# Node features of a graph kernel loaded on two queues, and the last rows of h stored on GpSimd's

## The chip, the cores and the metric

The kernel runs on one core of a Trainium2 chip. The metric is device microseconds (us) of one execution; below 4023 us, about 8 us are 0.2%. Engines are named as in the profile: PE is TensorE, DVE is VectorE, ACT is ScalarE, POOL is GpSimd, SP is SyncE. SPq and ACTq are the instruction queues of SP and ACT when they issue transfers.

## The reference, cut to what matters

One layer of a graph network with 12,500 nodes of 160 features (64 scalars, 32 vectors of 3 components) and 400,000 edges sorted by destination, then a residual and a layer norm.

```python
s = node_features[:, :64]; v = node_features[:, 64:].reshape(n, 32, 3)
h_s = s @ lin1_ws * a / sqrt(64)                                 # the table h, one row of 160 a node
h_v = einsum('nci,cd->ndi', v, lin1_wv) * a / sqrt(32)
w = silu(edge_scalars @ fc_w1 / sqrt(64)) @ fc_w2 / sqrt(64)     # 224 weights an edge
es, ev = h_s[edge_src], h_v[edge_src]                            # gathered by the edge's source
# messages: products of w, es, ev and edge_attr; summed by the edge's destination
# lin2 on the sums + a self connection -> gates -> out
x = layernorm(x + out)
```

Every edge needs the finished row of h of its source node, which can be any of the 12,500.

## The kernel before

**Set-up.** The table h is built in seven chunks of up to 2048 nodes (`CH`; `starts` holds their first nodes; the last chunk has 212). `load(c0)` (L229) loads a chunk, feature by feature, in three transfers: 64 scalar rows of 8 KB into partitions 0 to 63 of `xa` (512 KB, L235), the first 64 of the 96 rows of vector components into partitions 64 to 127 of `xa` (512 KB, L236), and the other 32 as four quarters into 128 partitions of `xz` (256 KB, L241). All three are issued by SP. ACT's queue brings the node attribute `at` (L249), the block-diagonal weights `l1` (L253, L256) and `l1z` (L277, four small strided transfers) and one row of destinations (L282). ACT also scales `l1` and `l1z` (L280).

The chunk loop (L309) does for each chunk: 16 matmuls with `l1` into the PSUM tiles `hp` (L320; 32 in the trace, since the profile shows two passes of a float32 matmul), four with `l1z` into `pz` (L336), and on DVE five multiplications by the attribute into `ht` (L323, L339). `hp` has six buffers, `ht` three, so a chunk's `ht` waits for the store of the chunk three before. POOL stores the chunk to the DRAM table `h_tab` (L350). Ahead of the fourth chunk, `bases()` (L292) computes each block's first destination on DVE, spreads it over the partitions by PE, and ACT copies it out of three `hp` buffers (L304). The last chunk is one full tile of 128 nodes, stored by POOL (L350), and 84 rows more, stored by SP (L353).

After the loop POOL issues the first edge scalars `es` (L196) and all destinations `dt` (L357); DVE scales `w2` (L364), computes the relative destinations `rel` (L398) when `dt` has landed, and runs `scale()` (L259) over the output weights, which SP loads at L368 to L391.

**Edge loop.** 782 steps of up to four tiles of 128 edges. POOL issues one indirect transfer a tile, which gathers 128 rows of `h_tab` into `hg` (L452; buffers for four steps). PE makes the edge weights (L443, L465), DVE the products (L475, L483) and the selection (L528, L537), PE adds them up by destination (L544), and closed blocks go through lin2 and the output steps. The order on PE, DVE, ACT and POOL is the order of the program text; SP's is too during the set-up (`tc.manual_schedule`). Transfers issued by SP and ACT share eight semaphores in turn, so a transfer waits until the one that last used its semaphore has landed.

Of the kernel before, what the change touches and what calls it, by code (L numbers as in the profile page):

```python
# [10 lines left out]
F32 = mybir.dt.float32  # L11
# [9 lines left out]
P = 128  # L21
S = 64
V = 32
# [30 lines left out]
def gnn_kernel(  # L54
# [21 lines left out]
    nc = tc.nc  # L76
# [10 lines left out]
    consts = ctx.enter_context(tc.tile_pool(name="consts", bufs=1))  # L87
    dram = ctx.enter_context(tc.tile_pool(name="dram", bufs=1, space=bass.MemoryType.DRAM))
    h_tab = dram.tile([N, D], F32, name="h_tab")
# [69 lines left out]
    def index(t):  # L159
        a0, idx, _ = ahead(t)  # L160
        return idx[:, t - a0:t - a0 + 1]
# [20 lines left out]
    def in_pairs(a):  # L182

        return a.rearrange("o (c k h) -> o h c k", k=KB, h=2)
# [11 lines left out]
            queue.dma_start(to[:, :n * P], es_t[:, e0:e0 + n * P])  # L196


    ident = consts.tile([P, P], F32, name="ident")
    make_identity(nc, ident)  # L200
    iota_i = consts.tile([P, W], I32, name="iota_i")
# [21 lines left out]
    starts = list(range(0, N, CH))  # L223
    with tc.tile_pool(name="nodes", bufs=len(starts)) as nodes, tc.tile_pool(
        name="nodes_ps", bufs=6, space=PSUM
    ) as nps, tc.tile_pool(name="z_ps", bufs=2, space=PSUM) as zps:
        loaded = []

        def load(c0):  # L229

            cn = min(CH, N - c0)
            quarters = 4 if cn == CH else 1
            assert quarters == 4 or cn <= U * P
            xa = nodes.tile([P, CH], F32, name="xa")
            nc.sync.dma_start(xa[:S, :cn], xs_t[:, c0:c0 + cn])  # L235
            nc.sync.dma_start(xa[S:, :cn], xv_t[:2 * V, c0:c0 + cn])  # L236
            xz = nodes.tile([P, U * P], F32, name="xz")
            cq = cn // quarters
            z = xv_t[2 * V:, c0:c0 + cq]
            if quarters == 4:  # L240
                nc.sync.dma_start(xz[:, :cq], bass.AP(tensor=z.tensor, offset=z.offset,  # L241
                                                      ap=[[z.ap[0][0], V], [cq, 4], [1, cq]]))
            else:
                nc.sync.dma_start(xz[S:S + V, :cq], z)
            loaded.append((c0, cn, quarters, cq, xa, xz))

        load(starts[0])
        at = consts.tile([P, NT], F32, name="at")
        nc.scalar.dma_start(at, attr)  # L249

        l1 = consts.tile([P, P], F32, name="l1")
        nc.vector.memset(l1, 0.0)
        nc.scalar.dma_start(l1[:S, :S], lin1_ws)  # L253
        for i in range(2):
            r = slice(S + i * V, S + (i + 1) * V)
            nc.scalar.dma_start(l1[r, r], lin1_wv)  # L256
        scales = [(l1[:S], 1.0 / math.sqrt(S)), (l1[S:], 1.0 / math.sqrt(V))]

        def scale():  # L259
            for m, by in scales:  # L260
                nc.vector.tensor_scalar_mul(m, m, by)
            scales.clear()

        def block_diagonal(name, w, n, scale, queue=nc.scalar):
            k = w.shape[0]
            m = consts.tile([n * k, n * k], F32, name=name)
            nc.vector.memset(m, 0.0)
            for i in range(n):
                queue.dma_start(m[i * k:(i + 1) * k, i * k:(i + 1) * k], w)
            if scale != 1.0:  # L270
                scales.append((m, scale))
            return m

        l1z = consts.tile([P, P], F32, name="l1z")
        nc.vector.memset(l1z, 0.0)
        for q in range(4):
            nc.scalar.dma_start(l1z[q:q + 4 * V - 3:4, q * V:(q + 1) * V], lin1_wv)  # L277
        scales.append((l1z, 1.0 / math.sqrt(V)))
        for m, by in scales:
            nc.scalar.mul(m, m, by)  # L280
        scales.clear()
        nc.scalar.dma_start(dt[0:1], dst[0:1])  # L282
        for c0 in starts[1:]:
            load(c0)
        index(0)
        raw = ends_pool.tile([2 * S, NWT], F32, name="raw")
        for half in range(2):
            r = slice(half * S, (half + 1) * S)
            nc.sync.dma_start(w1[r, r], fc_w1)
            nc.sync.dma_start(raw[r], fc_w2)  # L290

        def bases():  # L292

            firsts = dt[0:1, 0:(even - 1) * BT + 1:BT].rearrange("o (c h k) -> o h c k", k=KB, h=2)
            for half in range(2):
                nc.vector.tensor_copy(in_pairs(rows[:, :even])[:, half], firsts[:, half])
            nc.vector.tensor_copy(rows[:, even:], dt[0:1, even * BT:(NB - 1) * BT + 1:BT])
            base_f = ends_pool.tile([1, NB], F32, name="base_f")
            nc.vector.tensor_copy(base_f, rows)
            for b0 in range(0, NB, U * P):  # L300
                b1 = min(NB, b0 + U * P)
                ps = nps.tile([P, U, P], F32, name="hp").rearrange("p u c -> p (u c)")
                nc.tensor.matmul(ps[:, :b1 - b0], ones, base_f[:, b0:b1], start=True, stop=True)
                nc.scalar.copy(lo[:, b0:b1], ps[:, :b1 - b0])  # L304
            nc.vector.tensor_sub(share, rows, share)
            nc.vector.tensor_reduce(early, share, AX.X, OP.min)
            nc.vector.tensor_scalar(early, early, -float(MARGIN), None, op0=OP.is_lt)

        for c0, cn, quarters, cq, xa, xz in loaded:  # L309
            if c0 == 3 * CH:  # L310
                bases()
            ht = nodes.tile([P, 4 * U, D], F32, name="ht", bufs=3)
            nt = -(-cn // P)
            first = c0 // P
            full = cn // P
            for t0 in range(0, nt, U):
                ps = nps.tile([P, U, P], F32, name="hp")
                for t in range(t0, min(t0 + U, nt)):
                    n = min(P, cn - t * P)
                    nc.tensor.matmul(ps[:n, t - t0], xa[:, t * P:t * P + n], l1,  # L320
                                     start=True, stop=True)
                k = min(U, full - t0)
                nc.vector.tensor_mul(  # L323
                    ht[:, t0:t0 + k, :P], ps[:, :k],
                    at[:, first + t0:first + t0 + k, None].to_broadcast([P, k, P]))
                if t0 + k < nt <= t0 + U:
                    n = cn - full * P
                    nc.vector.tensor_scalar(ht[:n, full, :P], ps[:n, full - t0],
                                            at[:n, first + full:first + full + 1], None, op0=OP.mult)

            pz = zps.tile([P, U, 4, V], F32, name="pz")
            r = slice(0, P) if quarters == 4 else slice(S, S + V)
            by = l1z if quarters == 4 else l1[r, r]
            for u in range(-(-cq // P)):
                n = min(P, cq - u * P)
                nc.tensor.matmul(pz[:n, u, :quarters].rearrange("p q c -> p (q c)"),  # L336
                                 xz[r, u * P:u * P + n], by, start=True, stop=True)
            if quarters == 4:
                nc.vector.tensor_mul(  # L339
                    ht[:, :, P:].rearrange("p (q u) c -> p u q c", q=4), pz,  # L340
                    at[:, first:first + 4 * U].rearrange("p (q u) -> p u q", q=4)[:, :, :, None]
                    .to_broadcast([P, U, 4, V]))
            else:
                nc.vector.tensor_mul(ht[:, :full, P:], pz[:, :full, 0],
                                     at[:, first:first + full, None].to_broadcast([P, full, V]))
            if cn > full * P:
                n = cn - full * P
                nc.vector.tensor_scalar(ht[:n, full, P:], pz[:n, full, 0],
                                        at[:n, first + full:first + full + 1], None, op0=OP.mult)
            nc.gpsimd.dma_start(  # L350
                h_tab[c0:c0 + full * P, :].rearrange("(q p) d -> p q d", p=P), ht[:, :full])
            if cn > full * P:
                nc.sync.dma_start(h_tab[c0 + full * P:c0 + cn, :], ht[:n, full])  # L353


    load_chunk(0, nc.gpsimd)
# [26 lines left out]
    for to, part, pieces, w, r0, c0, by in maps:  # L383
        for k, piece in enumerate(pieces):
# [3 lines left out]
            m = terms.setdefault((to, part, four), len(terms))  # L388
# [267 lines left out]
    with tc.tile_pool(  # L656
        name="fin", bufs=1
    ) as fin, tc.tile_pool(
        name="late", bufs=2
    ) as late, tc.tile_pool(name="edge", bufs=2) as edge, tc.tile_pool(  # L660
        name="deep", bufs=4
# [150 lines left out]
        with tc.manual_schedule(engines={ENG.PE, ENG.DVE, ENG.Activation, ENG.Pool}):  # L812
# [47 lines left out]
            n = len(steps)  # L860
# [138 lines left out]
```

## Time and profile before

| | |
|---|---|
| three runs | 4021.55, 4023.07, 4029.47 us; median 4023.07 |
| the profiled execution | 4018.78 us, of which the span of the profile is 4017.0 us |
| granted PE clock, mean over the span | 0.967 |
| busy | PE 3676.3 us (92%), POOL 2982.9 (74%), DVE 2410.5 (60%), ACT 938.7 (23%) |
| gathers (L452) | 3125, each 950 ns; the first starts at 65.42 us, the last at 3984.85 us |

Times are us from the start of the span unless marked ns. In the list of instruction groups a line gives the source line, engine, operation, output<-input, count, then busy time and mean ns of one, then the idle time just before them and what ended most of it. In the timeline a line gives the start, the time taken, engine, line, operation, tiles, and in brackets the idle time before it with what released it. A row of DMA_DIRECT2D is the issue of a transfer and not its data; a transfer's landing is its semaphore's last update in the trace. In the table of stretches a line gives the stretch and its length, each engine's busy time with its number of instructions, the granted PE clock, the mean busy share of the 16 DMA engines, and GB/s.

### The profile page before, as it was taken

The page shows a single profiled execution, that of the slowest core. Times are in us where ns is not written, and L with a number is a line of the kernel's source. Part 1 is how long each engine was busy: PE and PEld are TensorE (multiplying, and loading weights), DVE is VectorE, ACT ScalarE, POOL GpSimd, SP SyncE. Part 2 cuts the span into 40 slices and gives each one's busy share as a digit, 9 for nine tenths or more (in the row PEclk, how much of TensorE's full clock was granted, in tenths as well). Part 3 has the DMA queues.
Part 4 walks back from the last instruction along what each step waited for, and adds up shares of the span by engine and source line. Part 5 has one row for each costly group of instructions (what it writes and reads, how often), then busy time and mean ns, then how long its engine had stood idle before and what let it go on. Part 6 is the DMA issues. An engine that isn't in the chain of part 4 may idle for free. (4 is left out here: it accounts for less than half of the span.)

```text
span 4017.0 us, 46675 instructions
## 1 busy us (share of the span) xinstructions
PE 3676.3 (92%) x14291; PEld 1588.0 (40%) x14291; DVE 2410.5 (60%) x6596; ACT 938.7 (23%) x2463; POOL 2982.9 (74%) x3144
## 2 busy tenths in 40 slices
PE   6899899999999999999999999999899989999997
PEld 4344343343343433334333443344343334333443
DVE  5556565655655655656656655666565665655655
ACT  2222222221222222212212222222121221222222
POOL 4777777777777777777777777777777777777775
PEclk8999999999999999999999999999999999999999
DMA  8444444443444444444444444444444444444442
GB/s 240 95 100 98 98 104 96 103 106 94 101 102 98 103 98 102 103 100 101 101 99 100 95 106 101 96 106 99 98 105 95 105 102 95 103 101 98 100 96 58
DMA packets 227691, 411.71 MB, mean 102 GB/s; under 512 B 71883, under 2 KB 157383, under 8 KB 226535
## 3 DMA queue, kind: packets, MB, share of 16 engines
q0 software_dynamic: 152272, 266.53, 27.9%
q1 hardware_dynamic: 74646, 142.01, 14.7%
q8 instruction: 115, 1.88, 0.2%
q14 instruction: 144, 1.18, 0.1%
q10 hardware_dynamic: 514, 0.10, 0.0%
HBM read 392.41 MB, written 16.00 MB: 102 GB/s over the span
## 5 line engine op out<-in xcount | busy, mean ns | idle before, releaser
L452 POOL DMA_INDIRECT hg<-h_tab,idx x3125 | 2968.7, 950 | 962.2 <-issue 865.5
L465 PE MATMUL pw<-w,hid 128*128 128x448 f32 x3126 | 1376.5, 564 | 191.5 <-DVE sel L537 150.1
L544 PE MATMUL pa<-pr,sel 128*64 128x416 f32 x6250 | 1303.5, 539 | 0.0
L475 DVE TENSOR_TENSOR pr<-pw,hg 128x512 f32<-128x512 f32 x782 | 540.5, 691 | 1042.4 <-DMA hg<-h_tab,idx 784.2
L483 DVE TENSOR_TENSOR pr<-pw,hg 128x384 f32<-128x384 f32 x2346 | 1153.6, 547 | 0.0
L465 PEld LDWEIGHTS pw<-w,hid 128*128 128x128 f32 x3126 | 556.3, 195 | 685.8 <-issue 445.3
L544 PEld LDWEIGHTS pa<-pr,sel 128*64 128x64 f32 x6250 | 388.0, 139 | 812.3 <-issue 799.4
L740 ACT COPY sa<-pa 128x416 f32<-128x416 f32 x521 | 263.1, 505 | 1415.4 <-PE pa L544 1413.0
L443 PE MATMUL misc<-es,w 128*128 128x512 f32 (+1 forms) x784 | 448.0, 654 | 17.0 <-DMA es<-in_es_t_dram 14.3
L528 DVE TENSOR_TENSOR pw<-rel,iota 128x64 f32<-128x64 int16 x782 | 178.4, 228 | 468.3 <-PE pw L465 465.5
L445 ACT ACTIVATE hid<-misc 128x512 f32<-128x512 f32 x392 | 233.5, 596 | 743.9 <-PE misc L443 743.4
L553 PEld LDWEIGHTS misc<-ident,sa 128*128 128x128 f32 x2084 | 239.6, 141 | 311.6 <-issue 252.1
L568 PE MATMUL misc<-tt,l 128*96 128x256 f32 (+5 forms) x1496 | 346.0, 378 | 1.7 <-ACT tt L558 1.5
L553 PE MATMUL misc<-ident,sa 128*128 128x128 f32 x2084 | 328.1, 280 | 0.9 <-DVE acc L721 0.8
L537 DVE TENSOR_TENSOR sel<-pw,eas 128x256 f32<-128x256 f32 x782 | 323.6, 414 | 0.0
L556 ACT COPY tt<-misc 128x192 f32<-128x192 f32 x521 | 164.5, 316 | 517.2 <-PE misc L553 516.7
L568 PEld LDWEIGHTS misc<-tt,l 128*96 128x96 f32 (+1 forms) x1496 | 227.0, 162 | 139.6 <-issue 72.6
L443 PEld LDWEIGHTS misc<-es,w 128*128 128x128 f32 x784 | 119.2, 191 | 283.2 <-issue 228.5
L576 DVE TENSOR_TENSOR acc<-acc,os 96x32 f32 x1042 | 195.6, 188 | 23.9 <-ACT os L571 5.5
L603 PE MATMUL misc<-ident,acc 96*128 96x96 f32 x196 | 36.4, 272 | 90.7 <-DVE pw L528 41.8
L558 ACT COPY tt<-misc 128x64 f32<-128x64 f32 x521 | 117.1, 225 | 0.0
L571 ACT COPY os<-misc 96x512 f32<-96x512 f32 (+2 forms) x68 | 38.3, 563 | 303.1 <-PE misc L568 280.4
(84 smaller groups left out, 653.0 us busy)
## 6 DMA issues: line engine op xcount, KB each, us to landing
es<-in_es_t_dram SPq DMA_DIRECT2D x258, 384.0 KB
hg<-h_tab,idx POOLq DMA_INDIRECT x3125
h_tab<-ht POOLq DMA_DIRECT2D x6, 1280.0 KB
xt<-in_x_dram SPq DMA_DIRECT2D x23, 320.0 KB
out_dram<-y SPq DMA_DIRECT2D x23, 320.0 KB
xv<-in_xv_t_dram SPq DMA_DIRECT2D x25, 187.5 KB
xs<-in_xs_t_dram SPq DMA_DIRECT2D x25, 125.0 KB
xa<-in_xs_t_dram SPq DMA_DIRECT2D x6, 512.0 KB
```

What stands on the lines that cost most here:

```text
L443: nc.tensor.matmul(ph[:k, c], w1[:k, :k], es[:k, t0 * P + c0 * P:t0 * P + c1 * P], start=True, stop=True)
L445: nc.scalar.activation(hid[:k, c], ph[:k, c], AF.Silu, scale=1.0 / math.sqrt(64))
L452: nc.gpsimd.indirect_dma_start(out=hg[:, t, :], out_offset=None, in_=h_tab, in_offset=bass.IndirectOffsetOnAxis(ap=i, axis=0))
L465: nc.tensor.matmul(pw[:, t:t + m, :NWT], hid[:m * S, c * P:(c + 1) * P], w2[:m * S, :m], start=True, stop=True)
L475: nc.vector.tensor_mul(two, pw[:, :n, :2 * S].rearrange("p t (k c) -> p t k c", k=2), hg[:, :n, None, :S].to_broadcast([P, n, 2, S]))
L483: nc.vector.tensor_mul(pr[:, :n, first:first + V3].rearrange("p t (i c) -> p t i c", i=3), pw[:, :n, None, 2 * S + k * V:2 * S + (k + 1) * ...
L537: nc.vector.tensor_mul(sel[:, :n], oh[:, :, None, :].to_broadcast([P, n, 4, W]), by_slot(tiles[0][0])[:, u:u + n, :, None].to_broadcast([P ...
L544: nc.tensor.matmul(pa[half * ROWS:(half + 1) * ROWS, :NPR], sel[:, t].rearrange("p k w -> p (k w)"), pr, start=start, stop=stop)
L553: nc.tensor.transpose(pt[:, four * P:four * P + k], sa[:k, c:c + P], ident[:k, :k])
L568: nc.tensor.matmul(po[:, k, :nb], l2[r, terms[to, part, four]], a[:, :nb], start=(n == 0), stop=(n == len(of) - 1))
L576: nc.vector.tensor_add(window, window, os[:, :, b])
L740: nc.scalar.copy(sa, pas.pop(j)[:, :NPR])
```

## The change

It has five edits. The vector half of `xa` is issued by ACT where SP issued it. `l1` and `l1z` are allocated and cleared at the head of the set-up. `l1` is scaled by `scale()` on DVE just ahead of the chunk loop; `l1z` stays with ACT, now after the second chunk's load. The loads of the other chunks follow that. The 84 last rows of h are stored by POOL right after the tile before them.

```diff
+    l1 = consts.tile([P, P], F32, name="l1")
+    l1z = consts.tile([P, P], F32, name="l1z")
+    for m in (l1, l1z):
+        nc.vector.memset(m, 0.0)
     ident = consts.tile([P, P], F32, name="ident")
...
             nc.sync.dma_start(xa[:S, :cn], xs_t[:, c0:c0 + cn])
-            nc.sync.dma_start(xa[S:, :cn], xv_t[:2 * V, c0:c0 + cn])
+            nc.scalar.dma_start(xa[S:, :cn], xv_t[:2 * V, c0:c0 + cn])
...
-        l1 = consts.tile([P, P], F32, name="l1")
-        nc.vector.memset(l1, 0.0)
         nc.scalar.dma_start(l1[:S, :S], lin1_ws)
...
-        l1z = consts.tile([P, P], F32, name="l1z")
-        nc.vector.memset(l1z, 0.0)
         for q in range(4):
             nc.scalar.dma_start(l1z[q:q + 4 * V - 3:4, q * V:(q + 1) * V], lin1_wv)
-        scales.append((l1z, 1.0 / math.sqrt(V)))
-        for m, by in scales:
-            nc.scalar.mul(m, m, by)
-        scales.clear()
         nc.scalar.dma_start(dt[0:1], dst[0:1])
-        for c0 in starts[1:]:
+        load(starts[1])
+        nc.scalar.mul(l1z, l1z, 1.0 / math.sqrt(V))
+        for c0 in starts[2:]:
             load(c0)
...
+        scale()
         for c0, cn, quarters, cq, xa, xz in loaded:
...
             if cn > full * P:
-                nc.sync.dma_start(h_tab[c0 + full * P:c0 + cn, :], ht[:n, full])
+                nc.gpsimd.dma_start(h_tab[c0 + full * P:c0 + cn, :], ht[:n, full])
```

## The prediction, made before the change was run

> **What bounds the kernel now.** I read the list of groups first, then who waited for whom on POOL, then the timeline of the first 85 us, then the DMA rate by stretch. The group that matters is the gather:
>
> ```profile
> L452 POOL DMA_INDIRECT hg<-h_tab,idx x3125 | 2968.7, 950 | 962.2 <-issue 865.5
> ```
>
> Each gather takes 950 ns and about 0.30 us of idle stands before it. POOL's waits, longest first, say what that idle is:
>
> ```profile
> POOL hg L452 <- issue: 865.5, 2841, 0.3
> ...
> POOL hg L452 <- DMA h_tab<-ht: 10.5, 1, 10.5
> ```
>
> The columns are total us, times, longest. No wait of a gather is longer than 0.3 us except the very first, which waited 10.5 us for h. The starts of the 3125 gathers run from 65.42 to 3984.85 us, a mean step of 1.2546 us, and the products (L483) free a gather's buffers at least 4.8 us before POOL needs them (81.81 against 86.58 us at the fifth step, the tightest of all). So PE's 92% does not set the pace: POOL's issue does, from the first gather to the last, and 31.2 us of output steps follow (4017.0 less 3984.85 and 0.95). This change touches nothing inside that loop. Its worth is how far it moves the first gather from 65.42 us, and 0.2%, about what a measurement of this kernel can tell from no change, is 8.0 us. The timeline shows what that start hangs on:
>
> ```profile
> 9.40 0.64 ACT L280 ACTIVATE l<-l 64x128 f32<-64x128 f32 x2
> 10.09 5.78 PE L320 MATMUL hp<-l,xa 128*128 128x128 f32 x32 [10.09 <-ACT l L280]
> 17.26 3.81 PE L320 MATMUL hp<-l,xa 128*128 128x128 f32 x32 [0.49 <-DMA xa<-in_xv_t_dram]
> 22.89 3.81 PE L320 MATMUL hp<-l,xa 128*128 128x128 f32 x32 [0.93 <-DVE ht L339]
> 41.77 1.15 POOL L350 DMA_DIRECT2D h_tab<-ht  x1 [11.87 <-DVE ht L339]
> 50.70 1.15 POOL L350 DMA_DIRECT2D h_tab<-ht  x1 [3.31 <-DVE ht L339]
> 52.71 0.56 POOL L350 DMA_DIRECT2D h_tab<-ht  x1 [0.85 <-DVE ht L348]
> 53.22 0.82 SPq L353 DMA_DIRECT2D h_tab<-ht  x1
> 65.42 1.04 POOL L452 DMA_INDIRECT hg<-h_tab,idx  x1 [10.52 <-DMA h_tab<-ht]
> ```
>
> PE begins at 10.09 us, when ACT has scaled `l1`; the second chunk waits for its vector half, and the third starts at 22.89, 0.09 us after its own vector half landed (22.80 by the semaphores). The last big store is issued until 51.85 and lands at 59.92, the 80 KB behind it at 60.38; but SP's 84 rows, issued at 53.22, land only at 64.47, and the gather follows 0.95 us later. The DMA rates of four stretches:
>
> ```profile
> 18.00:24.00 6.00, 5.07 (x46) 4.91 (x45) 3.46 (x5) 0.00 (x0) 2.19 (x2) 1.00 1.05 232
> 28.00:34.00 6.00, 3.26 (x6) 1.49 (x6) 5.08 (x8) 0.58 (x1) 1.28 (x1) 0.77 1.03 350
> 46.00:52.00 6.00, 4.60 (x41) 4.33 (x40) 3.37 (x7) 0.00 (x0) 2.30 (x2) 1.00 1.05 388
> 64.00:66.20 2.20, 1.33 (x2) 0.50 (x2) 0.00 (x0) 0.00 (x0) 0.78 (x1) 0.50 0.98 403
> ```
>
> The last two columns are busy share and GB/s. Loads of 64 partitions alone hold the DMA engines busy and move 232 GB/s; with stores beside them 350 to 388; `dt`, 128 partitions on one queue, 403. Busy is not full.
>
> **The change part by part.** All times are of the profiled execution (4018.78 us, 4.29 below the median of the three runs); I take the difference and subtract it from the median.
>
> *The 84 rows.* SP's queue is 4.1 us late against POOL's (64.47 against 60.38), because scattered small loads are ahead of it. On POOL's queue the rows follow 80 KB that land at 60.38; 54 KB at the 320 GB/s of the last stores are 0.2 us. POOL issues one more transfer: 0.56 us by the row at 52.71, ahead of `es` and `dt`, whose data wait behind stores until 59 us anyway. That backlog hides it; were the queue empty, it would cost 0.56. SP loses an issue of 0.82 us and a wait for DVE, and the output weights queued behind it come sooner. Gain 3.8 us, between 3.3 and 4.1.
>
> Does the rest keep up? `dt` stays 8.4 us behind the last big store (68.31 against 59.92) and the first products 13.5 us behind `dt` (81.81), so the fifth step's slack of 4.8 us shrinks by 3.8 to 1.0. It still covers; if it did not, POOL would wait the missing part once.
>
> *An earlier first matmul.* Gone from in front of it: ACT's table load (1.28 us, at 8.10, after ACT's issues), and 0.64 us of ACT multiplications. Added: one transfer issue (0.58) ahead of `at` and the weights on ACT's queue, and two DVE multiplications at about 0.21 us each (the nearest row is L261, 96x96). The memsets that hold `l1`'s transfer until 2.94 now come first on DVE, which starts at 0.82 us, so ACT issues `xv` 0.76, `at`, then `l1` from 1.8 to 3.4 against 4.57 now. The `l1` transfers landed at 8.8, 4.2 us after their issue; `at` landed 1.5 us after its own. Landing is then 4.9 to 7.6, and beyond if the small transfers take turns with the 512 KB ones on their queue and beside it, up to 9.0. I take 7.3, near the row of the same transfers, and 7.9 for PE: gain 2.2, between 0.5 and 4.5.
>
> *The load waits.* The second and third chunks lose 0.5 and 0.9 us to their loads. With the halves on two queues these go if the rate rises from 232 towards the 388 that two queues reach now: 1.28 MB are then 3.4 us a chunk, against 4.5 us of PE (3.65 + 0.97). Gain 1.4; nothing if the rate stays.
>
> A page speaks against this part: the Trainium skill's DMA: Bandwidth & Descriptors, Rules for kernel authors, says that two transfers to disjoint partition halves serialize on the same 16 engines and that spreading over issuing engines does not help bandwidth. SBUF — State Buffer, Door 1, says that partitions 0 to 63 reach only half of the ports, which would leave the other half free for the vector rows. By the first rule the sum below would be 1.4 smaller, by the second it stands; the 232 against 403 GB/s at equal busy share fits the second, and no run here shows two load queues.
>
> So the third chunk ends 3.6 us earlier, 24.7 for 28.32. *`bases()` and the fourth chunk* took 13.15 us from there (28.32 to 41.47), DVE and PE at a granted clock of 0.5 from 31.2; the same follows. Chunks five and six are 4.45 us each by the issue of their stores, PE-bound, so the last big store's issue ends at 48.25. ACT's five remaining load issues, about 0.6 us each, stand ahead of its copies at L304, which now start at 32.30: some 4 us of slack as long as the loads are not late. `l1z` is scaled on ACT after the second load; it is needed only after 5.8 us of matmuls.
>
> *The store's own backlog.* Stores run without a gap from 24.8 to 59 us, the first three at half rate beside the loads. With the loads over earlier the last big store meets an empty queue: about 2 us until data move (the fourth store's followed its issue within 2.3), 4.1 us of data, 0.7 to land: 6.8 for 8.07. Gain 1.3; it is 0 if the 5 us that the first store's data took to start is the rule.
>
> Sum: 3.8 + 2.2 + 1.4 + 1.3 = 8.7 us; the first gather at 56.7. The loop and the tail are taken as they are, at nothing. Profiled execution 4010.1, median 4014.4. All low ends together give 3.8, the high ends 11.3. The transfers set another limit: 17 MB up to the last row of h at 388 GB/s are 44 us, so it can't land before 46, which caps the whole gain near 17.
>
> **The rivals.** *Two queues are no faster.* For: the engines are busy all of 18 to 24 us. Against: 403 GB/s at the same share. Then the loads pace the first chunks as now, the early start is spent waiting, and mostly the 84 rows remain, with a part of the start: 4 to 6 us, 4018. *More than summed.* The idle before `bases()` falls differently and the fourth chunk sees the full clock: its matmuls took 5.71 us against 3.74 later, so 2 to 4 us more, 4011. For: the clock dropped at 31.2 and `bases()` now starts ahead of that. Against: the drop followed an idle of 3 us, which stays. *Slower.* ACT can't do L304 before it has issued the seventh vector load, and each load waits for a semaphore of an earlier one, SP's included. SP issued that load at 31.63 now. If the shared semaphores hold it back, L304 and the fourth chunk, whose fourth `hp` needs a buffer from L304, follow. The gain of the start is gone when that issue passes 32, all gain from 36, and it is slower than can be told from no change beyond 44; at 46 it would be 4033. Against: loads can only be held back by loads, and they start sooner.
>
> **How the numbers follow.** Forecast (gain 6 to 12): 0.62; two queues no faster (3 to 6): 0.22; more than summed (12 to 17): 0.09; slower: 0.07. The forecast straddles the line at 8.0 us: I put 0.46 of its 0.62 above, since 8.7 is above it and the mid of the unknown terms is not lower, 0.16 below. Faster 0.46 + 0.09 = 0.55, same 0.16 + 0.22 = 0.38, slower 0.07. Range: 4006 (the cap of 17) to 4021 (half the 84 rows), which leaves out the slower case and little else.
>
> **What would show it.** In the changed profile: first matmul near 8 us on DVE's `l1`; no L320 waiting for `xa`; a rate above 300 GB/s before the first store; L350's last big issue near 47; the first gather near 57, within 2 us of the last landing on POOL's queue; steps of 1.25 us as before. Wrong if the first gather starts after 60, if POOL waits at the fifth step for L483 by more than 1 us, or if L304 starts behind 32.

## The result and the profile after: slower by 8 us

The changed kernel took 4033.86 us (median of 17 runs, 4030.27 to 4037.48), the kernel before 4025.70 (17 runs beside it, 4019.44 to 4033.12): a ratio of 1.0020, 95% interval 1.0013 to 1.0027. That is slower by about 8 us, just on the line that was set for what can be told from no change, with an interval that leaves out no change. The forecast had 4014.4, and its range of 4006 to 4021 does not hold the time.

The profiled execution of the change took 4037.48 us (span 4035.6), the slowest of its 17; that of before, 4018.78, lies below the fastest of its own. So the two traces differ by 18.6 us of span, more than the medians. What the change did is read at the first gather: 73.92 us against 65.42, 8.5 us later, as the medians are 8.2 apart. Of the other 10, 6.2 us are the mean step of the gathers, 1.2566 against 1.2546 us 3124 times, and 3.9 lie behind the last gather; both are in code that the change does not touch. The group of gathers, answering to L452 of before:

```profile
L451 POOL DMA_INDIRECT hg<-h_tab,idx x3125 | 2973.9, 952 | 958.7 <-issue 866.2
```

Busy time, idle and its cause are those of before within 0.4%: POOL's issue still paces the loop. What differs is the start. Two lines of the timeline of before, for the block bases and the fourth chunk:

```profile
32.30 0.58 ACT L304 COPY lo<-hp 128x512 f32<-128x512 f32 x1 [21.93 <-PE hp L303]
...
34.15 5.71 PE L320 MATMUL hp<-l,xa 128*128 128x128 f32 x32
```

The timeline of the changed kernel:

```profile
0.76 0.56 ACTq L240 DMA_DIRECT2D xa<-in_xv_t_dram  x1
...
6.02 4.36 ACTq L277 DMA_DIRECT2D l1z<-in_lin_wv_dram  x4
...
12.23 0.22 DVE L263 TENSOR_SCALAR l<-l 64x128 f32<-64x128 f32 x1 [1.68 <-DMA l<-in_lin_wv_dram]
...
12.51 5.92 PEld L319 LDWEIGHTS hp<-l,xa 128*128 128x128 f32 x32 [12.51 <-DVE l L263]
...
17.96 30.81 ACTq L240 DMA_DIRECT2D xa<-in_xv_t_dram  x4
...
21.77 3.84 PE L319 MATMUL hp<-l,xa 128*128 128x128 f32 x32 [2.26 <-DMA xa<-in_xv_t_dram]
...
38.47 0.47 SPq L287 DMA_DIRECT2D w<-in_fc_w_dram  x1
...
48.81 1.15 ACT L302 COPY lo<-hp 128x512 f32<-128x512 f32 x3 [34.09 <-DMA raw<-in_fc_w_dram]
...
49.45 2.08 PE L319 MATMUL hp<-l,xa 128*128 128x128 f32 x8 [7.12 <-ACT lo L302]
...
54.26 1.15 POOL L349 DMA_DIRECT2D h_tab<-ht  x1 [20.99 <-DVE ht L338]
...
65.72 0.57 POOL L352 DMA_DIRECT2D h_tab<-ht  x1
...
73.92 1.04 POOL L451 DMA_INDIRECT hg<-h_tab,idx  x1 [6.00 <-DMA h_tab<-ht]
```

Three places carry the loss. PE begins at 12.51 us, not at 10.09: the vector part of `l1` came late, and DVE scaled it until 12.45. The second chunk waited 2.26 us for its vector half, where it had waited 0.49, and starts 4.5 us later than before (17.26). Then the copies of `lo`, L304 before and L302 now, start at 48.81 instead of 32.30. They stand on ACT behind the last load that ACT issues, and PE, which had started the fourth chunk at 37.77 and done 24 of its 32 matmuls, stood still for 7.12 us until a copy freed a PSUM buffer. The fourth store is issued 12.5 us later than before (54.26 against 41.77), and the fifth chunk loses another 0.8 us, so the last big store is issued 13.3 us late (64.02 against 50.70). At the end 4.8 us come back: from that issue to the first gather pass 9.90 us, and it was 14.72. 13.3 less 4.8 is the 8.5 us at the first gather.

The longest wait of ACT, and its columns are the total, the times and the longest one:

```profile
ACT lo L302 <- DMA raw<-in_fc_w_dram: 34.1, 1, 34.1
```

Most of the 34.1 us are no loss, since ACT had nothing to do before PE's sums for the block bases; a run below, in which DVE makes the copies, starts them at 35.95, so some 13 us are. No copy reads `raw` or `w`, the weights of the small network over the edge scalars, which SP loads at L288 and L287. What waits is the load ahead of the copies on ACT. Each load of SP and ACT signals its end on one of eight semaphores, and a later load on either queue that is given the same one is issued only once the earlier load has landed. In the trace's semaphore updates, ACT's sixth half, issued at 40.32, got the semaphore of an `xz` load that SP had issued at 24.47 and that landed at 40.30; the seventh got that of a 16 KB load of `w`, which SP issued at 38.47 and which landed at 48.28. The seventh half went out at 48.30, and the copies followed 0.5 us later.

And the rate did not rise. Three stretches of the changed kernel; the last columns are the granted PE clock, the busy share of the DMA engines, and GB/s:

```profile
2.00:10.00 8.00, 0.00 (x0) 0.00 (x0) 0.94 (x1) 0.00 (x0) 3.38 (x2) 1.00 1.04 230
18.00:24.00 6.00, 3.74 (x34) 3.55 (x33) 2.67 (x5) 0.00 (x0) 1.39 (x1) 1.00 1.04 234
34.00:50.00 16.00, 8.78 (x32) 6.55 (x33) 4.55 (x6) 1.15 (x3) 0.00 (x0) 0.62 0.93 319
```

In the first stretch both queues load at once, the scalar half on one and the vector half on the other, until the vector half has landed at 5.93 us; from 2.00 to 5.80 us the rate was 229 GB/s at a busy share of 1.02. The engines were as busy as before and moved the 232 GB/s of one queue.

### The profile page after: what moved, and what is told of

It is laid out like the page before. It is cut to its first block, busy times and chain, and to the rows that moved or that the text cites. A ratio compares the mean times of both kernels' runs of the same rounds, so it can differ in the third digit from the quotient of the medians.

```text
span 4035.6 us, 46675 instructions
## 1 busy us (share of the span) xinstructions
PE 3680.2 (91%) x14291; PEld 1592.3 (39%) x14291; DVE 2411.8 (60%) x6598; ACT 938.3 (23%) x2461; POOL 2988.7 (74%) x3145
```

## The experiments

All twelve ran on three other chips of the same kind, where the kernel before took a median of 5189, 5091 and 5171 us at a mean granted clock of 0.87 to 0.88 against 0.967 here, and where most of the time that the gathers wait is for the products (1229.8 us in the run with the 84 rows alone, against 871.6 for the issue); totals there say little about a few us. The set-up carries over: with its load order as before, the first matmul came at 10.06 us (10.09) and the copies at 32.28 (32.30), in the run with the 84 rows alone. So I compare the time from the start of the span to the first gather, 65.42 us before and 73.92 with the change, and give ratios where runs were timed. Two kernels were profiled twice, and their first gathers differ by 1.8 us (the change, 73.92 and 72.14) and 3.2 us (one transfer, 53.80 and 56.95); a difference of less than some 3 us between two single profiles shows nothing by itself.

### Which edit costs: the change with the vector half on SP

```diff
-            nc.scalar.dma_start(xa[S:, :cn], xv_t[:2 * V, c0:c0 + cn])
+            nc.sync.dma_start(xa[S:, :cn], xv_t[:2 * V, c0:c0 + cn])
```

> The changed kernel with one part undone: the vector half of xa is issued by SP again; weights first, l1 scaled on DVE, and the 84 rows on POOL stay. Theory 'ACT's order' (ACT's copies of the block bases, and behind them PE's fourth chunk, wait until ACT has issued its last vector half, and that issue waits for semaphores of SP's transfers): no copy waits behind a load any more, the copies start near 30 us, PE begins near 8 us, the first gather starts at 57 to 60 us against 73.9 in the changed kernel and 65.4 before; the whole 5 to 9 us below before. Rival 'DMA share' (a third stream of transfers slows the loads and stores, so the chunks' data come late whoever issues them): also better than the changed kernel, but only to the rate of before, first gather 61 to 65 us. Should the 84 rows on POOL's queue be what costs, the first gather stays above 65.

First gather 61.68 us; 5160.33 us, ratio 0.9961 (0.9929 to 0.9992). From the timeline of this run:

```profile
8.57 5.54 PE L319 MATMUL hp<-l,xa 128*128 128x128 f32 x32 [8.57 <-DMA l1z<-in_lin_wv_dram]
...
31.61 0.59 ACT L302 COPY lo<-hp 128x512 f32<-128x512 f32 x1 [21.02 <-PE hp L301]
...
33.45 6.71 PE L319 MATMUL hp<-l,xa 128*128 128x128 f32 x32
...
61.68 1.04 POOL L451 DMA_INDIRECT hg<-h_tab,idx  x1 [6.76 <-DMA h_tab<-ht]
```

One queue name makes the difference between 73.92 and 61.68. The copies wait for PE again, and at the old time. But 57 to 60 was missed: PE starts 1.5 us earlier than before, and by the fourth store this is gone (issued at 42.08; 41.77 before). The fourth chunk's 32 matmuls took 6.71 us against 5.71, at a granted clock of 0.50 from 32 to 38 us:

```profile
32.00:38.00 6.00, 6.00 (x25) 5.21 (x24) 1.38 (x2) 0.86 (x3) 0.00 (x0) 0.50 1.04 381
```

### The 84 rows alone, and the halves alone

The kernel before, with only the rows moved:

```diff
-                nc.sync.dma_start(h_tab[c0 + full * P:c0 + cn, :], ht[:n, full])
+                nc.gpsimd.dma_start(h_tab[c0 + full * P:c0 + cn, :], ht[:n, full])
```

> The kernel before with one part of the change done alone: the last 84 rows of h are stored by POOL. By the prediction's step: the first gather at 61.6 us for 65.4, 3.3 to 4.1 us gained on the whole, nothing else moved. Rival: POOL's extra issue and its place ahead of es and dt cost as much as the late landing on SP's queue did: first gather within 1 us of 65.4.

First gather 62.12 us, 3.3 earlier than before; 5177.24 us, ratio 0.9975 (0.9943 to 1.0006), which can't be told from none.

```profile
62.12 1.04 POOL L452 DMA_INDIRECT hg<-h_tab,idx  x1 [6.82 <-DMA h_tab<-ht]
```

The row move gains what it should: the first gather follows the landing of the last big store by 1.89 us (60.23 to 62.12), and it was 5.50 (59.92 to 65.42). Of the 3.7 us that the run ahead gained, this is most.

The kernel before, with only the vector halves moved:

```diff
-            nc.sync.dma_start(xa[S:, :cn], xv_t[:2 * V, c0:c0 + cn])
+            nc.scalar.dma_start(xa[S:, :cn], xv_t[:2 * V, c0:c0 + cn])
```

> The kernel before with one part of the change done alone: the vector half of xa is issued by ACT, ahead of the attribute and the weights for the first chunk. Theory 'ACT's order': ACT's copies of the block bases start behind its last load, later than 40 us against 32.3, the first matmul is later than 12 us against 10.1, and the first gather is at 74 to 80 us; the whole 8 to 14 us slower than before. Rival 'the weights' order' (the moved scaling of l1 and l1z and the 84 rows are what costs): the first gather within 3 us of 65.4.

First gather 70.95 us, 5.5 later than before; 5191.47 us, ratio 1.0010 (0.9982 to 1.0038). Smaller than expected, but with the same late copies behind the same kind of load:

```profile
44.70 1.15 ACT L304 COPY lo<-hp 128x512 f32<-128x512 f32 x3 [29.13 <-DMA w<-in_fc_w_dram]
```

The halves alone cost 5.5 us and the rest of the change gains 3.7, which would leave 1.8 together; the change lost 8.5. So the parts do not add. In this run the 84 rows, still on SP's queue, were no longer late: the first gather follows the landing of POOL's last store by 1.0 us (69.91 to 70.95), and it was 5.0 before (60.38 to 65.42). What moving them gains alone is not there to be gained. And the copies start 4.1 us earlier than in the change (44.70 against 48.81), behind another load; that the rest of the change, which rewrites the order of ACT's loads, makes this difference is likely, but no run shows it.

### Is it the copies behind the load? Copies on DVE, and two halves fewer on ACT

The change, with the copies taken from ACT:

```diff
-                nc.scalar.copy(lo[:, b0:b1], ps[:, :b1 - b0])
+                nc.vector.tensor_copy(lo[:, b0:b1], ps[:, :b1 - b0])
```

> The changed kernel with one thing taken from ACT: the copies of the block bases out of PSUM are done by DVE, so they cannot stand behind ACT's load issues; every transfer is as in the changed kernel. Theory 'ACT's order': PE's wait of 7.1 us for that copy goes, the fourth chunk goes on at about 43 us instead of 49.5, and the first gather moves from 73.9 to 65 to 69 us (the sixth chunk's vector half, landed at 47.6, and the seventh's, at 49, can then become the limit). Rival 'DMA share': the copies run earlier but the first gather stays within 1.5 us of 73.9.

First gather 64.90 us; 5174.50 us, ratio 0.9979 (0.9951 to 1.0008). All of ACT's loads are as late as in the change, only nothing that PE needs stands behind them:

```profile
35.95 0.69 DVE L302 COPY lo<-hp 128x512 f32<-128x512 f32 x1 [1.28 <-PE hp L301]
...
37.80 6.12 PE L319 MATMUL hp<-l,xa 128*128 128x128 f32 x32
...
64.90 1.04 POOL L451 DMA_INDIRECT hg<-h_tab,idx  x1 [5.92 <-DMA h_tab<-ht]
```

The fourth chunk runs through without a break. Of the 12.2 us between the change and its version with the halves on SP, the late copies are 9.0 (73.92 less 64.90), and the remaining 3.2, by difference, the late first chunks.

The change, with the last two of the seven vector halves on SP:

```diff
-            nc.scalar.dma_start(xa[S:, :cn], xv_t[:2 * V, c0:c0 + cn])
+            (nc.sync if c0 >= 5 * CH else nc.scalar).dma_start(xa[S:, :cn], xv_t[:2 * V, c0:c0 + cn])
```

> The changed kernel with only the last two vector halves (sixth and seventh chunk) issued by SP; the first five stay on ACT. Theory 'ACT's order': the copies follow PE at once, near 36 us for 48.8, the fourth chunk is not interrupted, first gather 63 to 67 us for 73.9, while the first matmul stays at 12.5. Rival 'two load queues are slow by themselves': first gather above 70.

First gather 65.50 us; one run, 5124.93 us.

```profile
36.45 0.59 ACT L302 COPY lo<-hp 128x512 f32<-128x512 f32 x1 [21.92 <-PE hp L301]
...
65.50 1.05 POOL L451 DMA_INDIRECT hg<-h_tab,idx  x1 [6.32 <-DMA h_tab<-ht]
```

Two loads less on ACT's queue, the two that had waited, bring the copies from 48.81 to 36.45 and give 8.4 us back. Both runs point to the same place by different edits.

### Are the two losses one? The first half on SP

The change, with the first vector half alone on SP, to take 512 KB from in front of the weights:

```diff
-            nc.scalar.dma_start(xa[S:, :cn], xv_t[:2 * V, c0:c0 + cn])
+            (nc.scalar if c0 else nc.sync).dma_start(xa[S:, :cn], xv_t[:2 * V, c0:c0 + cn])
```

> The changed kernel with only the first chunk's vector half issued by SP, so that ACT's queue begins with the attribute and the weights. Theory 'two costs' (512 KB ahead of the small weights delay the first matmul by some 4 us; ACT's last issues delay the copies and the fourth chunk by 7 or more): first matmul near 8.5 us for 12.5, the copies still later than 44 us, first gather 69 to 73 us for 73.9. Rival 'the start carries all': the whole set-up moves by 4 us and the first gather to 70 or below with the copies below 42.

A miss: the first gather came at 59.95 us (one run, 5156.17 us), and the late copies, which I had taken for a second and separate loss, were gone as well:

```profile
17.96 6.58 ACTq L240 DMA_DIRECT2D xa<-in_xv_t_dram  x3
...
31.38 0.59 ACT L302 COPY lo<-hp 128x512 f32<-128x512 f32 x1 [20.62 <-PE hp L301]
...
59.95 1.05 POOL L451 DMA_INDIRECT hg<-h_tab,idx  x1 [6.12 <-DMA h_tab<-ht]
```

ACT issued its last half by 24.54 us. By the trace's semaphores it now follows a half of ACT's own, issued at 9.78, and no longer a small weight of SP's. Which semaphore a load gets differs between the two kernels although the last loads stand on the same queues, so moving the first load has also changed what the last one waits for. With six of the seven halves still on ACT, the first gather came no later than with all of them on SP (61.68): a second load queue is no loss by itself.

With the first half and the last two on SP:

```diff
-            nc.scalar.dma_start(xa[S:, :cn], xv_t[:2 * V, c0:c0 + cn])
+            (nc.scalar if 0 < c0 < 5 * CH else nc.sync).dma_start(xa[S:, :cn], xv_t[:2 * V, c0:c0 + cn])
```

> The changed kernel with the first and the last two vector halves issued by SP, the second to the fifth on ACT: two load queues without the two places that cost. Theory 'two costs', with two queues no faster than one: first matmul near 8.5, copies at 31 to 35 us, first gather 60.5 to 63, as with all halves on SP (61.7). Rival 'two queues load faster once the waits are gone': first gather below 59.

First gather 60.94 us, copies at 32.26; one run, 5163.44 us. The numbers are those expected, though the run before had already refuted the theory of two costs, and no better than with the first half alone: once the last load is not held back, moving it gains nothing more. The change unaltered ran beside them:

> The changed kernel itself, unaltered, beside the others on the same chip: first gather at 73 to 75 us, copies of the block bases at 48 to 49, the whole 4 to 12 us above the kernel before. If the late copies were an accident of one execution, they start below 40 here.

First gather 72.14 us and copies at 47.77, each about 1 us ahead of what was expected; 5177.01 us, ratio 1.0013 (0.9987 to 1.0039), which can't be told from none.

```profile
47.77 1.15 ACT L302 COPY lo<-hp 128x512 f32<-128x512 f32 x3 [33.15 <-DMA raw<-in_fc_w_dram]
```

The late copies are no accident of one execution or one chip. What no run did was to give the last load a semaphore of its own and leave all else alone; that the semaphore is the link is read from the trace, while that the last loads and the copies behind them cost some 7 to 9 us is shown by two edits (64.90 and 65.50 against the 73.92 and 72.14 of the change).

### Why two queues are no faster: one transfer of 128 partitions

If 64 partitions set the 232 GB/s, a transfer of 128 should move more; if the 8 KB rows do, it should not. This is the version with the halves on SP, and both halves of `xa` in one transfer from an array in which the host has laid the scalar rows over the vector rows:

```diff
-            nc.sync.dma_start(xa[:S, :cn], xs_t[:, c0:c0 + cn])
-            nc.sync.dma_start(xa[S:, :cn], xv_t[:2 * V, c0:c0 + cn])
+            nc.sync.dma_start(xa[:, :cn], xa_t[:, c0:c0 + cn])
```

> As the run with the vector half back on SP, but the two halves of xa come in one transfer of 128 partitions (the host lays the two sources under each other); the same bytes in rows of the same 8 KB. Theory 'half width' (a transfer into 64 partitions moves about 230 GB/s, on one queue or on two, and one into 128 partitions moves more): more than 320 GB/s between the first and the second chunk, the waits of the second and third chunk for xa go, first gather 59 to 61 us against 61.7. Rival 'row length' (an 8 KB row takes a DMA engine 0.58 us whatever the partitions): the rate stays near 230 GB/s and the first gather within 1 us of 61.7.

First gather 53.80 us, earlier than either side had expected; one run, 5104.81 us. The stretch from 8 to 14 us, first with the two halves one after the other on SP, then with the one transfer:

```profile
8.00:14.00 6.00, 5.43 (x33) 5.46 (x34) 2.08 (x3) 1.59 (x2) 0.00 (x0) 1.00 0.96 225
```

```profile
8.00:14.00 6.00, 6.00 (x46) 6.00 (x45) 3.41 (x5) 1.13 (x2) 0.00 (x0) 1.00 1.01 393
```

The same rows of 8 KB, 225 against 393 GB/s at about the same busy share, and PE without a gap. In these stretches a packet of 8 KB, the row of one partition, takes an engine 0.57 us on average in the first (127 packets) and 0.32 in the second (228). So it is neither the length of the rows nor a fixed cost for each transfer, of which there are now half as many; it goes with the 64 partitions. The source array is another one, too, and no run separates that. Timed, the same kernel:

> The run with one transfer of 128 partitions for xa again, timed: the first gather at 53 to 55 us as in its first profile, the whole 8 to 15 us below the kernel before if the edge loop starts and ends that much earlier. Rival: the loop gives the start back (PE or DVE bound behind it): within 4 us of the kernel before.

First gather 56.95 us, 3 later than in its first profile and outside the 53 to 55 expected; why is not shown. 5147.17 us, ratio 0.9969 (0.9942 to 0.9996).

I also tried whether `bases()` between the chunks makes the gap ahead of the fourth. The version with the halves on SP, its DVE part at the second chunk, its PE and ACT part at the third, and the comparison with `share` after the loop:

```diff
-            if c0 == 3 * CH:
-                bases()
+            if c0 == CH:
+                base_f = bases()
+            if c0 == 2 * CH:
+                spread(base_f)
...
+        earliest()
```

> As the run with the vector half back on SP, but the block bases are computed on DVE after the first chunk, spread by PE after the second, and the check on them is done after the chunk loop, so that PE has no gap of some 3 us ahead of the fourth chunk. Theory 'gap and clock' (what the earlier start won was lost in that gap and in the half clock that follows it): the clock stays at 1.0 through the fourth chunk, its store is issued at 33 to 37 us for 42.1, first gather 54 to 59 us against 61.7. Rival 'transfers set the pace': the fourth chunk then waits for its loads and its ht buffer, first gather within 1.5 us of 61.7.

First gather 60.71 us, 1.0 earlier than without it, which is less than two profiles of one kernel differ by; one run, 5084.31 us. The copies were done at 23.3, yet DVE then waited 4.20 and 4.50 us for stores to free `ht`. So it is as the rival has it: with 64-partition loads the transfers set the pace. Both edits together:

> Both edits of the two runs before it: one transfer of 128 partitions for xa, the bases early, the vector rows not on ACT, the 84 rows on POOL. If both theories hold the chunks follow each other at 4.5 to 5 us, first gather 51 to 55 us, 10 to 14 us below the 65.4 of the kernel before; the whole faster by as much where the gathers pace the loop. If only one holds, 54 to 60.

First gather 53.35 us, loads at 408 GB/s from 8 to 14 us; 5071.04 us, ratio 0.9963 (0.9938 to 0.9989). This and the one transfer alone start the loop 8 to 12 us earlier than before and are faster than the kernel before on the chips that they ran on, the one transfer by an interval that only just leaves out no change; which of the two is better was not told apart, and neither ran on the chip of the result.

## Why the prediction was wrong, step by step

**What bounds the kernel: right.** The gathers pace the loop and the worth is the shift of the first one: 8.5 us there, 8.2 between the medians.

**The slack of ACT's copies: the step that failed.** The sum gave ACT's issues "some 4 us of slack as long as the loads are not late" and charged nothing. The price stood under the slower rival, from the right mechanism, and got 0.07 because "loads can only be held back by loads, and they start sooner". The first half of that sentence holds to the letter only: what held ACT's last issue back was a load, but 16 KB of the weight `w` and not one of the node features. The second half is no bound: SP issued this load at 38.47, behind its own waits, and it landed at 48.28. In place of the slack the copies started some 13 us late, PE stood still for 7.12 us, and the first gather lost some 7 to 9 us by the two runs that free the copies. The rival's scale was good: no gain from 36 and 4033 at 46. With the copies on DVE from 35.95 the first gather was within 0.6 us of before; with the issue at 48.30 the kernel took 4033.86. That these two times agree so well is in part luck: by the rival's own rate of 1 us for each us behind 36, an issue at 48.30 costs 12 us, and 8.2 were measured. PE had done 24 of the fourth chunk's 32 matmuls before it stood still. A wait that I had named, with a price above all the gain, had no bound from the trace of before, and I gave it odds by an argument.

**An earlier first matmul, 2.2: of the wrong sign.** 12.51 us against a forecast of 7.9. The upper end for the landing of `l1`, 9.0, was passed by 3 us: 512 KB now lead ACT's queue, the vector part landed at 12.1, and ACT's second half, behind the four `l1z` loads that were held at issue from 6.02 to 10.38, went out at 12.51, when the second of these had landed (12.49). With the halves on SP, PE did begin at 8.57, but those 1.5 us were worth nothing at the fourth store (42.08 against 41.77).

**The load waits, 1.4: nothing, the lesser bound.** From 232 to 403 GB/s at equal busy share I read rightly that 64 partitions go at little over half the rate, and wrongly that a second queue adds the other half; the 388 with stores beside loads was no row for two loads. Of the two rules that I weighed, that of the Trainium skill's DMA: Bandwidth & Descriptors, Rules for kernel authors, held: don't split over partition halves, they serialize; use one transfer of 128 partitions. The runs agree in both parts, with 230 GB/s on two queues and 393 to 408 in one transfer. Its reason, that both halves share the same 16 engines, does not by itself say why these engines move 393 GB/s in the other form; in these runs that stays open. SBUF — State Buffer, Door 1, says no more than that partitions 0 to 63 reach half of the ports, which no run here shows; that a second queue would then have the other half to itself was my inference and not the page's, and it is what failed. The 4.5 us of PE a chunk that the prediction sets against the loads are 4.62 by its own terms (3.65 + 0.97); nothing else rests on them.

**The 84 rows, 3.8: right, a little large.** Alone 3.3 us. Counted from the landing of the last big store to the first gather, 3.6 alone and 3.5 in the change (1.89 and 1.96 us for 5.50).

**The store's backlog, 1.3: it came.** From the end of its issue to its landing the last big store took 6.79 us in the change (65.17 to 71.96), where the sum had 6.8 for 8.07, and 7.05 with the halves on SP; with the 84 rows alone it took 7.96. With the 3.5 us of the rows this makes the 4.8 that come back at the end. The reason that was given, loads that are over earlier, is not tested: in the change it is the store that comes late.

**The fifth step's slack: close.** It was to shrink from 4.8 to 1.0 us, or else cost POOL what is missing, once. It went: POOL waited once for the products there, 0.8 us against 0.3 elsewhere, ahead of the gather at 95.81. That is 0.5 us. The first products came 13.5 us behind `dt`, as forecast, but `dt` landed 10.1 us behind the last big store (71.96 to 82.04) and not 8.4.

**The rivals.** Two queues no faster, 0.22, was true in its cause and wrong in its time: it left ACT's queue out. More than summed did not happen. Of the prediction's three signs of being wrong, "the first gather starts after 60" and "L304 starts behind 32" came, and both point to the step that failed; the wait at the fifth step stayed under 1 us.

## What to carry to other kernels

Before moving loads to a queue whose engine also computes, list what stands behind its last issue, and look up for each issue which earlier load on any queue shares its semaphore and when that one lands; a small transfer that is issued late can hold up a compute engine, here ACT from 40.8 to 48.3 us behind 16 KB. When a trace shows busy DMA engines at half the rate, widen the transfer to all partitions before spreading it over queues. And price a rival from a row of the trace before giving it odds: if no row bounds it, the range has to reach it.

## What was not expected of the hardware

Two load queues into disjoint halves of the partitions moved 230 GB/s together, as much as one, and one transfer over all 128 partitions 393 to 408. Three other chips ran the same kernel before in medians of 5091 to 5189 us against 4026 here, at a mean granted clock of 0.87 to 0.88 against 0.967, while the first matmul and the copies of the block bases, with the loads in the old order, came at the same times to 0.03 us. That the clock is the reason is not shown. In the twelve profiles from there, DVE waits 139 to 156 times ahead of the same instruction of the edge loop (L528 of before), for 1146 to 1249 us in all, for something that the profile calls only `remote`. The two profiles from the chip of the result have no such wait, and the sum is about what the medians differ by (1065 to 1163 us); what it is stays open.
